# Row statistics of two layer norms in a Mamba block with FFN: from VectorE to ScalarE's accumulator output

## The chip, the cores and the metric

The kernel runs on one core of one Trainium2 chip. The time is device microseconds (us) of one execution on that core, given as the median of three runs; a profiled execution is a further run, with its own time. Five engines are in play, and the text uses the profile's names for them: PE (TensorE, matmuls), DVE (VectorE), ACT (ScalarE), POOL (GpSimd) and SP (SyncE, which issues the DMAs).

## The reference

The input x has shape (4, 2048, 256). The output is one pre-norm layer, a Mamba block and then a gated FFN, each in a residual connection. The change concerns only the two layer norms outside of the blocks; a third norm stands inside the Mamba block, and the kernel folds it into the first one.

```python
def _layernorm(x, axis=-1, eps=1e-05):
    m = jnp.mean(x, axis=axis, keepdims=True)
    v = jnp.var(x, axis=axis, keepdims=True)
    return (x - m) / jnp.sqrt(v + eps)
...
# _mamba_block(x, ...): D_INNER = 512, D_STATE = 64
mu = jnp.mean(x, axis=-1, keepdims=True)
var = jnp.mean(jnp.square(x - mu), axis=-1, keepdims=True)
xn = (x - mu) * jax.lax.rsqrt(var + 1e-05) * ln_w + ln_b
xz = xn @ W_in                       # xi, z; causal conv of width 4 on xi; u = silu(conv)
x_dbl = u @ W_xproj                  # dt_r, Bm, Cm;  delta = softplus(dt_r @ W_dt + b_dt)
def step(h, inputs):                 # one time step: h is (batch, 512, 64)
    d_t, B_t, C_t, u_t = inputs
    dA = jnp.exp(d_t[:, :, None] * A)
    h = h * dA + (d_t * u_t)[:, :, None] * B_t[:, None, :]
    y_t = jnp.einsum('bdn,bn->bd', h, C_t)
    return (h, y_t)
...                                  # y = (ys + u * D) * silu(z); return residual + y @ W_out
...
x = x + mamba(_layernorm(x))
x = x + ffn(_layernorm(x))           # ffn: (silu(x @ wg.T) * (x @ wu.T)) @ wd.T, weights from integers
```

## The kernel before

**Tiles and groups.** The 4 x 2048 tokens are cut into 16 tiles of 512 tokens, four to a sequence. The recurrence of a tile runs in 16 groups of 16 scans, so 256 scans a tile and 4096 in all. One scan is one DVE instruction over 512 time steps for 128 rows (two channels by 64 states). A group goes through this pipeline, all of it in `group`:

- SP loads `d*u` of 16 channel pairs, broadcast over the states, into a buffer of `ring` (three buffers of 128 x 16 x 512); four DMAs a group.
- POOL multiplies the ring by B in two instructions of eight rows each (`mul`, line 1578). Before that it puts the carried state into the first column (line 1451).
- For each pair, PE spreads delta over the rows by a matmul into one of four PSUM buffers `a` (line 1461), ACT takes the exponential in place (line 1467), and DVE runs the scan (line 1472), reading `a` and the ring's row and writing the ring's row.
- After the group, PE contracts the states with C in 64 "narrow" matmuls of 32 columns to a block of PSUM (line 1496), ACT evicts them (line 1517), PE permutes (line 1530). Only when the narrow matmuls have read the whole buffer can the ring's buffer be loaded for the group after the next two.

**Dense work.** What is not the recurrence is called dense: for tile n+1 `front` (loads x, both norms' statistics as one, normalises, transposes), `front_a` (projection, convolution), `front_b` (projection of z, a block of three SiLU activations between two table loads at lines 947 to 950, softplus, stores of what the recurrence loads); for tile n-1 `back` (gate, output projection, residual, store of the sum x1 to DRAM, `rsum`) and `back_b` (loads x1 again, norm of the FFN, FFN with a SiLU block at lines 1198 to 1200, residual, store). All of it runs beside the scans of tile n. The first tile's front and the last tile's end (`back_early`, `back_last`) stand outside.

**The norm.** `layer_norm` takes for each of four blocks of 128 tokens a `bn_stats` over 256 values and a `bn_aggr` (lines 469 and 470, both DVE), which give mean and variance in a PSUM buffer `lp`. ACT adds eps (line 479), takes Ln and Exp (489, 490) and a square (491); three small DVE instructions (494, 499, 504) finish the reciprocal root by a Newton step and make the bias -mean times that. `normalise` (line 520) is one ACT instruction a block, with a scale and a bias from SBUF. The norm is called 16 times in `front` (with `twice=True`), 15 times in `back_b`, and twice for half a tile in `back_last`.

**The order.** No engine reorders its instructions. `Planner.run` writes the order of every queue when the kernel is built: it steps through the operations with a cost that the kernel states for each, places on each engine what can start first, and biases dense work by a due step. A changed cost or operation thus moves other operations too. PSUM has four buffers `ps` for everything but `a`; SBUF has four of `w4` and eight small ones `s4`. Where it judges that PE has had little work lately, the planner issues a matmul of line 1461 twice.

Of the kernel before, what the change touches and what calls it, by code (L numbers as in the profile page):

```python
# [15 lines left out]
AF = mybir.ActivationFunctionType  # L16
# [4 lines left out]
P = 128  # L21
# [35 lines left out]
TINY = 60  # L57
SWITCH = 90
PAD = 0.0
SLACK = {"DVE": 300.0, "POOL": 300.0}  # L60


# [29 lines left out]
class Planner:  # L92
# [13 lines left out]
    def buf(self, tag):  # L106
        tag, view = self.alias.get(tag, (tag, None))
        t = tag if tag in self.ordered else tag + self.kind
        b = Buf(tag, self.turns.get(t, 0), view)
        self.turns[t] = b.turn + 1  # L110
        return b
# [225 lines left out]
def mamba_ffn_kernel(  # L337
# [81 lines left out]
    def act(n=T, psum=False, ptr=0):  # L419
        return n * 0.834 + (70 if psum else 110) + 93 * ptr  # L420
# [23 lines left out]

        return t[:, b // 2, b % 2 : b % 2 + 2, :].rearrange("p a c -> p (a c)")

    def layer_norm(src, blocks=range(4), twice=False):

        nb = len(blocks)
        m = 2 if twice else 1
        lp, ve, rs, nm = buf("ps"), buf("s4"), buf("s4"), buf("s4")

        def sq():
            return lp.t[:, 16 : 16 + m * nb]

        def col(b):
            return b.t[:, 0 : m * nb]

        def mv():
            return lp.t[:, 0 : 2 * nb].rearrange("p (s c) -> p s c", c=2)

        def two(v):
            return v.rearrange("p (m s) -> p m s", m=m)

        def stats(j, s):
            st = buf("bst")
            op("DVE", 326, lambda: nc.vector.bn_stats(st.t, tok(src)[:, s, :]), [(src, s // 2)], [st])
            op("DVE", 205, lambda: nc.vector.bn_aggr(mv()[:, j, :], st.t), [st], [(lp, 0, j)])  # L470

        for j, s in enumerate(blocks):
            stats(j, s)
        mk = [(lp, 0, j) for j in range(nb)]

        def var(i):
            op(
                "ACT", 180,
                lambda: nc.scalar.activation(
                    ve.t[:, i * nb : (i + 1) * nb], mv()[:, :, 1], AF.Copy,  # L480
                    bias=EPS * EPS if i else EPS, scale=1.0 + EPS if i else 1.0,
                ),
                mk, [(ve, i)],
            )

        for i in range(m):
            var(i)
        vk = [(ve, i) for i in range(m)]
        op("ACT", 180, lambda: nc.scalar.activation(col(rs), col(ve), AF.Ln), vk, [rs])
        op("ACT", 180, lambda: nc.scalar.activation(col(rs), col(rs), AF.Exp, scale=-0.5), [rs], [rs])  # L490
        op("ACT", 180, lambda: nc.scalar.activation(sq(), col(rs), AF.Square), [rs], [(lp, 1)])
        op(
            "DVE", TINY,
            lambda: nc.vector.scalar_tensor_tensor(sq(), sq(), -0.5, col(ve), ALU.mult, ALU.mult),
            [(lp, 1)] + vk, [(lp, 1)],
        )
        op(
            "DVE", TINY,
            lambda: nc.vector.scalar_tensor_tensor(col(rs), sq(), 1.5, col(rs), ALU.add, ALU.mult),
            [(lp, 1), rs], [rs],  # L500
        )
        op(
            "DVE", TINY,
            lambda: nc.vector.scalar_tensor_tensor(  # L504
                two(nm.t[:, 0 : m * nb]), mv()[:, None, :, 0].to_broadcast([P, m, nb]), -1.0,
                two(rs.t[:, 0 : m * nb]), ALU.mult, ALU.mult,
            ),
            mk + [rs], [nm],
        )
        return rs, nm  # L510

# [193 lines left out]

    B2, yts, heads_in = {}, {}, {}

    rest, gates, last = {}, {}, {}

    def load_x(n):  # L710
        b, q = n // NQ, n % NQ
# [9 lines left out]
    def front(n):  # L721
        r = n % R
        xt = load_x(n) if n else x0
        rs, nm = layer_norm(xt, twice=True)
        rp = buf("s4")
        op("ACT", 180, lambda: nc.scalar.activation(rp.t[:, 0:4], rs.t[:, 0:4], AF.Copy, bias=1.0), [rs], [rp])
        xn = buf("w4")
        normalise(xn, xt, (rs, nm), o=4)

        def keep():  # L730
            normalise(xt, xt, (rp, nm))
            store(rsum[r], lambda: tok(xt), 524288, halves(xt), [("rsum", r)])

        if n:
            keep()
        else:
            last["keep"] = keep
        xnT = buf("w4")

        def ev_t(c):  # L740
            def ev(ps):
                op(
                    "ACT", act(T, True, 2),
                    lambda: nc.scalar.activation(  # L744
                        xnT.t[:, c, :], ps.t, AF.Identity, bias=lnb[:, c : c + 1], scale=lnw[:, c : c + 1]
                    ),
                    [ps, "lnw", "lnb"], [(xnT, c)],
                )

            return ev  # L750

        for c in range(2):
            transposes(xn, c, ev_t(c))
        rest[n] = xnT
# [349 lines left out]
            ),  # L1104
        )

    def residual(pieces, reads, x1, h):

        ps = buf("ps")
        v = lambda: tok(x1)[:, h * 2 : h * 2 + 2, :].rearrange("p s c -> p (s c)")  # L1110
        open_bank(ps)
        op("ACT", act(), lambda: nc.scalar.copy(ps.t, v()), [(x1, h), ps], [ps])
        for cost, f in pieces:
            op("PE", cost, lambda f=f: f(ps.t), reads, [ps])
        op("ACT", act(T, True), lambda: nc.scalar.copy(v(), ps.t), [ps], [(x1, h)])

    def ev_add(x1, h):
        def ev(ps):
# [13 lines left out]
    def back(n):  # L1132
        r = n % R
        b, q = n // NQ, n % NQ
        y2 = buf("w8")
        for hf in range(2):
            for rh in range(2):
                ld = [buf(("yl", "w2")[rh]) for _ in range(2)]
                for _ in gate_y(n, y2, hf, rh, ld):
                    pass  # L1140
        x1 = buf("w4")
        load(lambda: tok(x1), rsum[r], 524288, r=[("rsum", r)], w=[(x1, 0), (x1, 1)])

        for h in range(2):
            yk = [(y2, hf, h) for hf in range(2)]
            residual(
                [mm_tok_add(wout, lambda k: y2.t[:, k, :], s, k, range(4)) for s in (2 * h, 2 * h + 1) for k in range(4)],
                yk + ["wout"], x1, h,
            )
        store(rsum[r], lambda: tok(x1), 524288, halves(x1), [("rsum", r)])  # L1150

    def back_b(n):
        r = n % R
        b, q = n // NQ, n % NQ
        x1 = buf("w4")
        load(lambda: tok(x1), rsum[r], 524288, r=[("rsum", r)], w=halves(x1))
        sc = layer_norm(x1)
        xn = buf("w4")
        normalise(xn, x1, sc)
        xT = buf("w4")  # L1160

        def ev_t(c):
            def ev(ps):
                op("ACT", act(T, True), lambda: nc.scalar.copy(xT.t[:, c, :], ps.t), [ps], [(xT, c)])

            return ev

        for c in range(2):
            transposes(xn, c, ev_t(c))
        hma, hmb = buf("w8"), buf("w4")  # L1170

        def hm(k):
            return hma.t[:, k, :] if k < 4 else hmb.t[:, k - 4, :]

        hk = [(hma, k) for k in range(4)] + [(hmb, k) for k in range(2)]

        def ev_g(k):
            def ev(ps):
                op("ACT", act(T, True), lambda: nc.scalar.copy(hm(k), ps.t), [ps], [hk[k]])

            return ev

        def ev_u(k):
            def ev(ps):
                up = buf("w2")
                op("ACT", act(T, True), lambda: nc.scalar.copy(up.t, ps.t), [ps], [up])  # L1186
                op(
                    "POOL", 1230, lambda: nc.gpsimd.tensor_tensor(hm(k), hm(k), up.t, ALU.mult),  # L1188
                    [up, hk[k]], [hk[k]],
                )  # L1190

            return ev

        for k in range(6):
            project(wgu, k * P, xT, ev_g(k), [("wgu", 0, k)])

        def silu():
            nc.scalar.activation(hma.t, hma.t, AF.Silu)
            nc.scalar.activation(hmb.t, hmb.t, AF.Silu)
            nc.scalar.preload_act_table_set(EXP_LN)  # L1200

        op("ACT", 5450, silu, hk, hk).tail = -1283.0
        for k in range(6):
            project(wgu, HID + k * P, xT, ev_u(k), [("wgu", 1, k)])
        wdk = [("wd", c, k) for c in range(2) for k in range(3)]
        for h in range(2):
            residual(
                [mm_tok_add(wd, hm, s, k, range(6)) for s in (2 * h, 2 * h + 1) for k in range(6)],
                hk + wdk, x1, h,
            )  # L1210
        store(
            out[b, q * T : (q + 1) * T, :].rearrange("(s p) c -> p s c", p=P), lambda: tok(x1), 524288,
            [(x1, 0), (x1, 1)], [],
        )
# [436 lines left out]
```

## Time and profile before

| | |
|---|---|
| median of three runs | 5000.17 us (4996.33 to 5005.06) |
| the profiled execution, its own time | 4990.98 us |
| its span in the profile | 4989.2 us |
| granted TensorE clock | 0.98 |
| DVE busy | 4758.8 us (95%) |
| POOL busy | 4697.7 us (94%) |
| PE busy | 4475.7 us (90%) |
| ACT busy | 3973.4 us (80%) |
| DVE scans, line 1472 | 4595.0 us, 4096 instructions |
| POOL multiplications, line 1578 | 4545.0 us, 512 instructions |
| DVE `bn_stats`, line 469 | 45.1 us, 128 instructions |
| DVE `bn_aggr`, line 470 | 21.8 us, 128 instructions |

Busy time is the time in which an engine runs at least one instruction; neighbours on one engine overlap a little, so an instruction's own duration (1195 ns for a scan) is longer than the distance to the next one. In the groups' lines, the columns are the line, engine, operation, output and inputs with shapes, the count, the busy time and mean duration, and the idle time of the engine just before, with what ended it. In the timeline each line has a start, a duration, the engine, line, operation and count of a run of equal instructions, and in brackets the idle time before it.

### The profile page before, as it was taken

What the parts mean: (1) busy time and instruction counts of PE and PEld (TensorE: products, weight loads), DVE (VectorE), ACT (ScalarE), POOL (GpSimd) and SP (SyncE); (2) the same over time, 40 slices, a digit from 0 to 9 for tenths busy, and PEclk for the clock granted to TensorE, in tenths of its full rate; (3) what the DMA queues carried; (4) which work ended last, traced back from release to release, by engine and by line L of the source; (5) the groups of instructions that cost most, each with busy time, mean ns of one, the idle gap of its engine ahead of it and who ended that gap; (6) DMA issues with size and microseconds to landing.
All of it is one profiled execution on the core that took longest, in us unless ns stands there. A gap on an engine that the chain in (4) does not pass through costs nothing.

```text
span 4989.2 us, 115894 instructions
## 1 busy us (share of the span) xinstructions
PE 4475.7 (90%) x46955; PEld 2171.1 (44%) x46955; DVE 4758.8 (95%) x4696; ACT 3973.4 (80%) x7138; POOL 4697.7 (94%) x862
## 2 busy tenths in 40 slices
PE   7889899899988989989998989989999898899888
PEld 2434344444444444444443434434444343444435
DVE  7999999999999999999999999999999999999996
ACT  6778878788787887878878787887878878788674
POOL 6999999999999999999999999999999999999994
PEclk9999999999999999999999999999999999999999
DMA  8676676666676767767667666667767677676762
GB/s 291 236 280 269 262 281 262 259 271 254 263 289 255 273 235 271 296 260 272 250 267 278 259 253 251 271 270 273 268 261 276 234 271 290 243 277 246 266 252 85
DMA packets 306346, 1299.86 MB, mean 261 GB/s; under 512 B 33617, under 2 KB 134737, under 8 KB 174866
## 3 DMA queue, kind: packets, MB, share of 16 engines
q1 hardware_dynamic: 305810, 1292.44, 67.3%
q8 instruction: 369, 6.05, 0.5%
q14 instruction: 167, 1.37, 0.1%
HBM read 1186.94 MB, written 105.38 MB: 259 GB/s over the span
## 4 chain that ended last, share of the span: by engine, by line
PE 41%; DVE 20%; ACT 15%; issue 10%; DMA 8%; POOL 5%; DVEq 0%; SPq 0%; POOLq 0%; ACTq 0%
DVE ring L1472 19%; PE a L1461 11%; PE ps L1496 9%; ACT a L1467 7%; PE ps L545 7%; DMA ring<-dusc 4%; PE ps L1097 4%; POOL ring L1578 4%; PE ps L779 3%; DMA yl<-qd 2%; PE ps L1530 2%; PE ps L898 2%; ACT mm L1517 1%; DMA dusc<-w 1%; PE ps L846 1%
## 5 line engine op out<-in xcount | busy, mean ns | idle before, releaser
L1578 POOL TENSOR_TENSOR ring<-ring,b 128x4088 f32<-128x4088 f32 (+2 forms) x512 | 4545.0, 8920 | 177.0 <-DMA ring<-dusc 110.3
L1472 DVE TENSOR_TENSOR_SCAN ring<-a,ring 128x512 f32<-128x512 f32 x4096 | 4595.0, 1195 | 104.9 <-ACT a L1467 62.5
L1467 ACT ACTIVATE a<-a,a 128x512 f32<-128x512 f32 x4096 | 2697.0, 665 | 707.3 <-PE a L1461 678.0
L1461 PE MATMUL a<-stk,selb 128*128 128x512 bf16 x5119 | 1806.7, 388 | 417.0 <-DVE ring L1472 376.5
L1496 PE MATMUL ps<-ring,cz 128*32 128x128 f32 x32768 | 1288.6, 279 | 11.1 <-issue 6.6
L1496 PEld LDWEIGHTS ps<-ring,cz 128*32 128x32 f32 x32768 | 786.3, 109 | 756.1 <-issue 699.2
L1461 PEld LDWEIGHTS <-selb 128*128 128x128 bf16 x5119 | 474.5, 98 | 1302.5 <-issue 1223.8
L545 PE MATMUL ps<-w,wgu 128*128 128x512 f32 x720 | 378.1, 608 | 0.0
L1517 ACT COPY mm<-ps 128x512 f32<-128x512 f32 x512 | 303.7, 593 | 53.0 <-PE ps L1496 52.0
L1530 PE MATMUL ps<-mm,exs 128*32 128x128 f32 (+1 forms) x4112 | 285.5, 407 | 5.8 <-ACT mm L1517 5.7
L545 PE MATMUL ps<-w,win 128*128 128x512 f32 x512 | 264.4, 601 | 0.3 <-ACT w L744 0.3
L779 PE MATMUL ps<-xi,w 128*128 128x512 f32 x480 | 248.6, 599 | 0.0
L1530 PEld LDWEIGHTS ps<-mm,exs 128*32 128x32 f32 x4112 | 117.3, 119 | 185.6 <-ACT a L1467 82.8
L1097 PE MATMUL ps<-wd,w 128*128 128x256 f32 x720 | 195.2, 387 | 0.0
L545 PEld LDWEIGHTS ps<-w,wgu 128*128 128x128 f32 x720 | 138.5, 194 | 103.9 <-issue 50.3
L1097 PEld LDWEIGHTS ps<-wd,w 128*128 128x128 f32 x720 | 132.5, 190 | 39.1 <-issue 12.7
L898 PE MATMUL ps<-w,ident 128*128 128x512 f32 x248 | 132.7, 618 | 2.8 <-ACT w L878 1.2
L1188 POOL TENSOR_TENSOR w<-w,w 128x512 f32<-128x512 f32 x90 | 114.6, 1301 | 16.0 <-ACT w L1186 15.8
L1097 PE MATMUL ps<-wout,w 128*128 128x256 f32 x480 | 128.8, 383 | 0.0
L545 PEld LDWEIGHTS ps<-w,win 128*128 128x128 f32 x512 | 96.6, 192 | 71.9 <-issue 48.8
L1041 PE MATMUL ps<-prm,yt 128*128 128x128 f32 x512 | 83.7, 294 | 34.6 <-ACT ps L1054 34.0
L520 ACT ACTIVATE w<-w,s,s 128x256 f32<-128x256 f32 x192 | 112.2, 592 | 1.9 <-DVE s L504 0.9
(147 smaller groups left out, 2381.9 us busy)
## 6 DMA issues: line engine op xcount, KB each, us to landing
ring<-dusc SPq DMA_DIRECT2D x1023, 1024.0 KB, 8.3
stk<-dsc SPq DMA_DIRECT2D x256, 96.0 KB, 5.5
qd<-w SPq DMA_DIRECT2D x32, 512.0 KB, 5.6
szd<-w SPq DMA_DIRECT2D x32, 512.0 KB, 8.3
dusc<-w SPq DMA_DIRECT2D x63, 256.0 KB, 3.6
dsc<-pk SPq DMA_DIRECT2D x63, 256.0 KB, 3.0
rsum<-w SPq DMA_DIRECT2D x31, 512.0 KB, 3.4
w<-rsum SPq DMA_DIRECT2D x31, 512.0 KB, 7.9
```

What stands on the lines that cost most here:

```text
L545: lambda ps: nc.tensor.matmul(ps, w[:, c, o : o + P], xT.t[:, c, :], start=(c == 0), stop=(c == 1)),
L779: lambda: nc.tensor.matmul(ps.t, dg.t[:, j * P : (j + 1) * P], xi.t[:, j : j + T], start=(j == 0), stop=(j == 3)),
L898: lambda: nc.tensor.matmul(ps.t, m, t.t, start=False, stop=True, skip_group_check=True),
L1097: lambda ps: nc.tensor.matmul(ps[:, (s % 2) * DM : (s % 2 + 1) * DM], src(k)[:, s * P : (s + 1) * P], w[:, k, :], start=False, stop=(k == ...
L1188: "POOL", 1230, lambda: nc.gpsimd.tensor_tensor(hm(k), hm(k), up.t, ALU.mult),
L1461: "PE", 216, lambda: nc.tensor.matmul(a.t, selb[:, p, :], stk.t, start=True, stop=True),
L1467: lambda: nc.scalar.activation(a.t, a.t, AF.Exp, scale=a2f[:, idx : idx + 1]), [a, "a2"], [a],
L1472: nc.vector.tensor_tensor_scan(v, a.t, v, 0.0, ALU.mult, ALU.add)
L1496: nc.tensor.matmul(pm.t[cg * 32 : cg * 32 + 32, (r8 % 4) * P : (r8 % 4 + 1) * P], framed(cz, blk), ring.t[:, :, blk * 8 : blk * 8 + 8], st ...
L1517: nc.scalar.copy(mm.t[:, hb * 4 : hb * 4 + 4].rearrange("p r a t -> p (r a t)"), pm.t)
L1530: nc.tensor.matmul(ex.t[jh * 32 : jh * 32 + 32, a * 16 : b * 16], framed(exs, jh * 2 + jl), mm.t[:, a:b, :, jh * 2 + jl], start=(jl == 0), ...
L1578: e.tensor_tensor(v, v, b2.t[:, None, t0:].to_broadcast([P, m, T - t0]), ALU.mult)
```

## The change

The fifteen inner tiles' norms of both kinds no longer use `bn_stats` and `bn_aggr`. ACT sums instead, by the output `accum_out` of an activation.

- In `front` of tiles 1 to 15, a new function `sums_of` runs four copies of a 128 x 256 block into a PSUM buffer that nobody reads, each with its row sums as a second output. `layer_norm` then scales the sums to -mean (one small ACT instruction) and runs four `Square` activations with -mean as a bias from SBUF, whose row sums are 256 times the variance.
- In `back` the eviction of the residual (two copies of 128 x 512) becomes four of 128 x 256 with row sums. The rest of the norm's scalars is worked out there, from x1 while it lies in SBUF; `back_b` only loads x1 and normalises.
- The first tile's front and the two half norms at the end stay as they are.
- The planner is told 60 ns more for an instruction with an accumulator output (`ACC`).

```diff
+ACC = 60.0
...
+    def sums_of(src):
+        sums = buf("s4")
+        sink = buf("ps")
+        def one(s):
+            op("ACT", act(DM) + ACC,
+                lambda: nc.scalar.activation(
+                    sink.t[:, 0:DM], tok(src)[:, s, :], AF.Copy, accum_out=sums.t[:, s : s + 1]),
+                [(src, s // 2)], [sink, (sums, s)])
...
-    def layer_norm(src, blocks=range(4), twice=False):
+    def layer_norm(src, blocks=range(4), twice=False, sums=None):
...
+        def spread(s):
+            op("ACT", act(DM, ptr=1) + ACC,
+                lambda: nc.scalar.activation(
+                    lp.t[:, DM : 2 * DM], tok(src)[:, s, :], AF.Square,
+                    bias=sums.t[:, 4 + s : 5 + s], accum_out=sq4.t[:, s : s + 1]),
+                [(src, s // 2), (sums, 4)], [(lp, 2), (sq4, s)])
...
+        if sums is None:
+            for j, s in enumerate(blocks):
+                stats(j, s)
+        else:
+            op("ACT", 180,
+                lambda: nc.scalar.activation(sums.t[:, 4:8], sums.t[:, 0:4], AF.Copy, scale=-1.0 / DM),
+                [(sums, s) for s in range(4)], [(sums, 4)])
+            for s in range(4):
+                spread(s)
...
     def front(n):
-        rs, nm = layer_norm(xt, twice=True)
+        rs, nm = layer_norm(xt, twice=True, sums=sums_of(xt) if n else None)
...
-    def residual(pieces, reads, x1, h):
+    def residual(pieces, reads, x1, h, sums=None):
-        op("ACT", act(T, True), lambda: nc.scalar.copy(v(), ps.t), [ps], [(x1, h)])
+        if sums is None:
+            op("ACT", act(T, True), lambda: nc.scalar.copy(v(), ps.t), [ps], [(x1, h)])
+            return
+        def one(i):
+            s = h * 2 + i
+            op("ACT", act(DM, True) + ACC,
+                lambda: nc.scalar.activation(
+                    tok(x1)[:, s, :], ps.t[:, i * DM : (i + 1) * DM], AF.Copy, accum_out=sums.t[:, s : s + 1]),
+                [ps], [(x1, h), (sums, s)])
...
     def back(n):
+        sums = buf("s4")
...
         store(rsum[r], lambda: tok(x1), 524288, halves(x1), [("rsum", r)])
+        norms[n] = layer_norm(x1, sums=sums)
     def back_b(n):
         load(lambda: tok(x1), rsum[r], 524288, r=[("rsum", r)], w=halves(x1))
-        sc = layer_norm(x1)
-        normalise(xn, x1, sc)
+        normalise(xn, x1, norms[n])
```

More of the change, by code (lines that the diff above doesn't have):

```diff
@@ L445, in framed @@
         return t[:, b // 2, b % 2 : b % 2 + 2, :].rearrange("p a c -> p (a c)")
-    def layer_norm(src, blocks=range(4), twice=False):
+    def sums_of(src):
+        sums = buf("s4")
+        sink = buf("ps")
+        def one(s):
+            op(
+                "ACT", act(DM) + ACC,
+                lambda: nc.scalar.activation(
+                    sink.t[:, 0:DM], tok(src)[:, s, :], AF.Copy, accum_out=sums.t[:, s : s + 1]
+                ),
+                [(src, s // 2)], [sink, (sums, s)],
+            )
+        for s in range(4):
+            one(s)
+        return sums
+    def layer_norm(src, blocks=range(4), twice=False, sums=None):
         nb = len(blocks)
         m = 2 if twice else 1
-        lp, ve, rs, nm = buf("ps"), buf("s4"), buf("s4"), buf("s4")
+        lp = buf("ps")
+        sq4 = buf("s4") if sums else None
+        ve, rs, nm = buf("s4"), buf("s4"), buf("s4")
         def sq():
@@ L470, in stats, with var_in, minus_mean @@
             op("DVE", 205, lambda: nc.vector.bn_aggr(mv()[:, j, :], st.t), [st], [(lp, 0, j)])
-        for j, s in enumerate(blocks):
-            stats(j, s)
-        mk = [(lp, 0, j) for j in range(nb)]
+        def spread(s):
+            op(
+                "ACT", act(DM, ptr=1) + ACC,
+                lambda: nc.scalar.activation(
+                    lp.t[:, DM : 2 * DM], tok(src)[:, s, :], AF.Square,
+                    bias=sums.t[:, 4 + s : 5 + s], accum_out=sq4.t[:, s : s + 1],
+                ),
+                [(src, s // 2), (sums, 4)], [(lp, 2), (sq4, s)],
+            )
+        if sums is None:
+            for j, s in enumerate(blocks):
+                stats(j, s)
+            mk = [(lp, 0, j) for j in range(nb)]
+        else:
+            op(
+                "ACT", 180,
+                lambda: nc.scalar.activation(sums.t[:, 4:8], sums.t[:, 0:4], AF.Copy, scale=-1.0 / DM),
+                [(sums, s) for s in range(4)], [(sums, 4)],
+            )
+            for s in range(4):
+                spread(s)
+            mk = [(sq4, s) for s in range(4)]
+        def var_in():
+            return mv()[:, :, 1] if sums is None else sq4.t[:, 0:4]
+        def minus_mean():
+            return mv()[:, None, :, 0] if sums is None else sums.t[:, None, 4:8]
         def var(i):
@@ L479, in var @@
                 lambda: nc.scalar.activation(
-                    ve.t[:, i * nb : (i + 1) * nb], mv()[:, :, 1], AF.Copy,
-                    bias=EPS * EPS if i else EPS, scale=1.0 + EPS if i else 1.0,
+                    ve.t[:, i * nb : (i + 1) * nb], var_in(), AF.Copy,
+                    bias=EPS * EPS if i else EPS, scale=(1.0 + EPS if i else 1.0) / (1 if sums is None else DM),
                 ),
@@ L504, in layer_norm @@
             lambda: nc.vector.scalar_tensor_tensor(
-                two(nm.t[:, 0 : m * nb]), mv()[:, None, :, 0].to_broadcast([P, m, nb]), -1.0,
+                two(nm.t[:, 0 : m * nb]), minus_mean().to_broadcast([P, m, nb]), 1.0 if sums else -1.0,
                 two(rs.t[:, 0 : m * nb]), ALU.mult, ALU.mult,
             ),
-            mk + [rs], [nm],
+            (mk if sums is None else [(sums, 4)]) + [rs], [nm],
         )
@@ L706, in mamba_ffn_kernel @@
     B2, yts, heads_in = {}, {}, {}
-    rest, gates, last = {}, {}, {}
+    rest, gates, norms, last = {}, {}, {}, {}
     def load_x(n):
@@ L1114, in residual @@
             op("PE", cost, lambda f=f: f(ps.t), reads, [ps])
-        op("ACT", act(T, True), lambda: nc.scalar.copy(v(), ps.t), [ps], [(x1, h)])
+        if sums is None:
[3 more added lines that the diff above has]
+            s = h * 2 + i
+            op(
+                "ACT", act(DM, True) + ACC,
+                lambda: nc.scalar.activation(
+                    tok(x1)[:, s, :], ps.t[:, i * DM : (i + 1) * DM], AF.Copy, accum_out=sums.t[:, s : s + 1]
+                ),
+                [ps], [(x1, h), (sums, s)],
+            )
+        for i in range(2):
+            one(i)
     def ev_add(x1, h):
@@ L1147, in back @@
                 [mm_tok_add(wout, lambda k: y2.t[:, k, :], s, k, range(4)) for s in (2 * h, 2 * h + 1) for k in range(4)],
-                yk + ["wout"], x1, h,
+                yk + ["wout"], x1, h, sums,
             )
         store(rsum[r], lambda: tok(x1), 524288, halves(x1), [("rsum", r)])
+        norms[n] = layer_norm(x1, sums=sums)
     def back_b(n):
```

## The prediction

> **What bounds the kernel now.** I read the page's busy shares first, then the groups by line, then the timelines of DVE and ACT over one inner tile, then who waited for whom.
>
> ```profile
> PE 4475.7 (90%) x46955; PEld 2171.1 (44%) x46955; DVE 4758.8 (95%) x4696; ACT 3973.4 (80%) x7138; POOL 4697.7 (94%) x862
> ```
>
> DVE is the fullest engine, POOL is almost as full. The groups say what fills DVE and what the change takes away:
>
> ```profile
> L1472 DVE TENSOR_TENSOR_SCAN ring<-a,ring 128x512 f32<-128x512 f32 x4096 | 4595.0, 1195 | 104.9 <-ACT a L1467 62.5 <-POOL ring L1451 34.5 <-POOL ring L1578 7.7
> L469 DVE BATCH_NORM_STATS2 bst<-w 128x6 f32<-128x256 f32 x128 | 45.1, 410 | 26.6 <-DMA w<-rsum 24.8 <-DMA w<-in 1.7
> L470 DVE BATCH_NORM_AGGREGATE ps<-bst 128x2 f32<-128x6 f32 x128 | 21.8, 170 | 1.3
> ```
>
> Read alone, this looks like 67 us of DVE work and 25 us of waiting for a reload to be had. The timeline shows where that work stands. First DVE, in two stretches of one tile, then ACT beside the first:
>
> ```profile
> 1324.40 74.77 DVE L1472 TENSOR_TENSOR_SCAN ring<-a,ring 128x512 f32<-128x512 f32 x67
> 1400.27 1.41 DVE L469 BATCH_NORM_STATS2 bst<-w 128x6 f32<-128x256 f32 x4 [1.09 <-DMA w<-rsum]
> 1403.69 22.39 DVE L1472 TENSOR_TENSOR_SCAN ring<-a,ring 128x512 f32<-128x512 f32 x20 [2.02 <-ACT a L1467]
> ...
> 1482.66 0.39 DVE L470 BATCH_NORM_AGGREGATE ps<-bst 128x2 f32<-128x6 f32 x2
> ...
> 1489.95 29.07 DVE L1472 TENSOR_TENSOR_SCAN ring<-a,ring 128x512 f32<-128x512 f32 x26
> 1518.95 0.47 DVE L1391 TENSOR_TENSOR ps<-ps,a 128x128 f32<-128x128 f32 x2
> 1519.33 1.39 DVE L469 BATCH_NORM_STATS2 bst<-w 128x6 f32<-128x256 f32 x4
> 1522.11 36.89 DVE L1472 TENSOR_TENSOR_SCAN ring<-a,ring 128x512 f32<-128x512 f32 x33 [1.39 <-ACT a L1467]
> 1560.54 17.94 DVE L1472 TENSOR_TENSOR_SCAN ring<-a,ring 128x512 f32<-128x512 f32 x16 [1.54 <-POOL ring L1578]
> ```
>
> ```profile
> 1395.72 0.67 ACT L1467 ACTIVATE a<-a,a 128x512 f32<-128x512 f32 x1
> 1396.41 1.28 ACT L947 ACT_TABLE_LOAD   x1
> 1397.71 1.91 ACT L947 ACTIVATE w<-w 128x2048 f32<-128x2048 f32 x1
> 1399.53 1.99 ACT L949 ACTIVATE w<-w 128x1024 f32<-128x1024 f32 x2
> 1401.53 1.28 ACT L950 ACT_TABLE_LOAD   x1
> 1402.83 0.27 ACT L1539 COPY yt<-ps 128x128 f32<-128x128 f32 x1
> ```
>
> Sixty-seven scans take 74.77 us, so one follows the other every (74.77 - 1.19) / 66 = 1.115 us. The scans are the spine: the first starts at 54.7 us, 4096 x 1.115 = 4567 us, the last ends at 4933.1 us, and 56 us of tail follow. That leaves 4989.2 - 54.7 - 4567 - 56 = 311 us in which DVE does something else between scans or waits. Only that can move.
>
> The SiLU block keeps ACT from exponentials from 1396.4 to 1402.8 us. DVE uses up the (at most four) finished `a` buffers, runs dry at 1399.2 and resumes at 1403.7: a hole of 4.5 us. All four `bn_stats` stand in it, the wait for the reload too, and DVE still waits 2.02 us for ACT after them. The second block (line 1198) makes a hole of about 3 us, and the front's four `bn_stats` stand there, again with ACT coming last. In the order of the instructions 29 of the 30 inner norms lie like this: their `bn_stats` follow the last scan whose exponential precedes a SiLU's table load.
>
> **The change part by part.** All terms stand against the profiled execution (4990.98 us); the median of the runs is 9.2 us above it, and I carry the difference over to the median.
>
> *The 120 `bn_stats` and the waits for the reload.* 42.3 us busy (45.1 x 120/128) and 24.8 us of waits, of which I count nothing as gain: the SiLU block covers them, and what comes next in the hole is ACT's exponential at the same moment as now. Without that cover they would be worth 67 us.
>
> *The 120 `bn_aggr`.* From 1482.66 to 1489.95 us, 7.29 us hold six scans (6.69 us), four `bn_aggr` and three small operations that stay; a scan with one of the latter takes 1.19 us instead of 1.115. So four `bn_aggr` cost 7.29 - 6.69 - 3 x 0.07 = 0.4 us, 30 norms 12 us. The front's stand between 1578 and 1593 us, where the rows around them wait 0.84 and 0.22 us for POOL; a faster DVE would wait longer there. Between 6 and 12 us, I take -9.
>
> *New work on ACT.* The trace has no accumulating activation. Nearest rows for the instruction itself: 0.37 us for a 128x256 copy (lines 1262 and 1277), 0.49 us for a 128x256 activation with one operand from SBUF (1054), 0.20 us for a tiny one. A front gets 4 x 0.37 + 4 x 0.49 + 0.20 = 3.6 us, a back 4 x 0.37 - 2 x 0.59 + 4 x 0.49 + 0.20 = 2.5 us; fifteen of each 92 us. The second output costs between nothing (the same pass over the data; it can't be less) and a small instruction of its own (0.19 us for 128x3, line 771): 240 times, 0 to 46 us. I take 20 us, nearer to the first, as nothing moves but one value a row. ACT goes from 3973 to some 4085 us, 82%. Is it on the path? In the new order the squares stand one behind each exponential: 0.60 + 0.49 + 0.02 to 0.19 us against a scan's 1.115 us, so at worst ACT falls back 0.2 us a block, 1.6 us a norm, against a lead of up to three scans (3.3 us). The norms stand 50 and more exponentials ahead of the SiLU blocks, and just ahead of those the new order has less dense work on ACT than the old. So 0; if the lead were gone, the 1.6 us of 30 norms would cost 48 us. The copies and squares use functions that lines 491 and 726 already run between the same table loads; no load is added.
>
> The Trainium skill speaks against this move: its page "ScalarE: Activation LUTs", section "Rules for kernel authors", says to put additions and multiplications on VectorE, which is the quicker engine for them. Rows agree on the engine time (1.41 + 0.4 us on DVE against 2.5 to 3.6 us on ACT), and if engine time were what counts, the sum would be 92 - 54 = 38 us slower, about 5038. But the rule weighs the engines as if both were on the path.
>
> *Waits that move.* The reload of x1 is now waited for by ACT's normalise, with the exponentials queued behind it; DVE waited up to 3.1 us for it. SP issues it at the same place of its queue, and on ACT the first normalise stands eight exponentials behind the SiLU block, over 8 us later than `bn_stats` stood. 0. `sums_of` holds one of four `ps` buffers for four copies, and `lp` is held through the squares; on SP no DMA is added or removed.
>
> *The moved order.* The planner's costs changed, so everything dense shifts: the order has 104 doubled matmuls of line 1461 fewer (104 x 0.39 = 40 us of PE, none on the path). What matters is when a group's narrow matmuls are through, since the reload of its ring buffer waits for the last. In the tile shown, the group whose scans end at 1540.9 had them through only at 1562.5, with FFN matmuls in between; POOL waited 4.2 us, and DVE then 1.54 us at 1560.54. DVE's waits for POOL are 34.5 + 7.7 = 42 us in all. Counted in matmuls of line 1461 between a group's end and its last narrow matmul, groups 12 and 13 of a tile go from 20.2 and 19.4 to 16.9 and 18.4, but groups 5 to 8 from 14.6, 13.5, 12.6, 14.6 to 19.0, 15.3, 13.5, 13.9; the mean goes from 14.4 to 14.0. Bounds: -42 us (all such waits gone) to +42 us (a second such place); I take -9, a fifth of the waits, as the worst place gets better and another nearly as bad appears.
>
> Sum: 0 - 9 + 0 - 9 = -18 us, so 4973 us for the profiled execution and 5000.2 - 18 = 4982 us for the median.
>
> **The rivals.**
>
> *Full relief.* DVE gets all of it: 42.3 + 12 + 24.8 = 79 us less, 4921 us. For it speaks the 95%; against it that the row after the stats waits for ACT, not the other way.
>
> *Nothing to measure.* The back's aggregates come (-6), the front's are lost to POOL, and the moved order takes a few us: 4990 to 5010 us.
>
> *Slower: PE late at a second place.* Groups 5 to 8 now have their narrow matmuls late. A buffer that is free d us after its group's scans end is loaded and landed 5 us later, POOL starts about 3 us after that and needs 8.9 us for the first half; two groups of scans give 2 x 17.9 = 35.7 us. So DVE waits once d exceeds some 19 us, counted here as about 19 matmuls, just where group 5 now stands. POOL is in order and has no reserve (94%), so a loss stays. Price: as at the present place, up to 42 us, with the gain from the aggregates 33 us net: 5010 to 5035 us.
>
> **How the numbers follow.** The likeliest case (4965 to 4990 us) gets 0.47, full relief 0.08, nothing 0.20, slower 0.25. A run of this kernel can be told from no change at about 0.2%, 10 us. Faster by more: 0.47 + 0.08, less 0.01 for the edge, 0.54; same 0.20; slower 0.26. Below 4960 us lies full relief and a corner of the likeliest (0.10), above 5028 us the upper part of the slower case (0.10); between them 0.8.
>
> **What would show it.** Right: the holes at the SiLU blocks keep their 4.5 and 3 us; DVE's wait for `a` from ACT rises from 62.5 us by about the removed 42 and 25 us, to some 125 us, while DVE busy falls to about 4700 us; ACT busy is 4065 to 4110 us; DVE's waits for POOL are some 33 us. Wrong: the holes shrink (full relief), the waits of line 1472 for POOL rise over 50 us (the slower rival), or waits for `a` appear away from the SiLU blocks, which would mean that accumulating costs ACT far more than 0.19 us.

## The result, and the profile after

The changed kernel takes 5204.61 us (median of four runs, 5182.04 to 5245.78) against 4999.86 us before (four runs): 1.0421 times as long, with a 95% interval of 1.0388 to 1.0453. That is 205 us slower, where 18 us faster was forecast and 5028 us was the upper end of the range. The profiled execution was the fastest of the four, 5182.04 us; its span is 5180.3 us.

First the busy shares on the page of the changed kernel:

```profile
PE 4464.3 (86%) x46549; PEld 2178.5 (42%) x46851; DVE 4883.3 (94%) x4456; ACT 4051.3 (78%) x7618; POOL 4695.3 (91%) x862
```

DVE has 240 instructions fewer (4456 against 4696) and is busy 124.5 us longer. So an instruction that stayed has become dearer. The groups by line, with different shapes kept apart, name it. The first two lines are of the kernel before, the last of the norm's three small operations (the 16 of the front include the first tile); the others are of the changed kernel, where the same operation stands in line 551:

```profile
L504 DVE SCALAR_TENSOR_TENSOR s<-ps,s 128x8 f32<-128x8 f32 x16 | 2.2, 139 | 0.0
...
L504 DVE SCALAR_TENSOR_TENSOR s<-ps,s 128x4 f32<-128x4 f32 x15 | 2.0, 133 | 0.0
```

```profile
L1535 DVE TENSOR_TENSOR_SCAN ring<-a,ring 128x512 f32<-128x512 f32 x4096 | 4593.8, 1197 | 170.3 <-ACT a L1530 135.9 <-issue 19.6 <-POOL ring L1514 10.9
...
L551 DVE SCALAR_TENSOR_TENSOR s<-s,s 128x8 f32<-128x8 f32 x15 | 104.0, 6934 | 0.2
...
L551 DVE SCALAR_TENSOR_TENSOR s<-s,s 128x4 f32<-128x4 f32 x15 | 72.3, 4822 | 0.0
```

An operation on four or eight values a row went from 0.14 us to 6.9 and 4.8 us: 176.3 us in 30 instructions. Its idle time before is nil, so by the column on the right it waits for nothing; the time lies inside of the instruction. The operands differ: `s<-ps,s` before (one input in PSUM), `s<-s,s` now (both in SBUF). The timeline shows what ends it. First DVE, then POOL in the same microseconds:

```profile
1071.53 1.21 DVE L1535 TENSOR_TENSOR_SCAN ring<-a,ring 128x512 f32<-128x512 f32 x1
1072.66 8.33 DVE L551 SCALAR_TENSOR_TENSOR s<-s,s 128x4 f32<-128x4 f32 x1
1080.92 2.33 DVE L1535 TENSOR_TENSOR_SCAN ring<-a,ring 128x512 f32<-128x512 f32 x2
```

```profile
1063.31 17.66 POOL L1641 TENSOR_TENSOR ring<-ring,b 128x4088 f32<-128x4088 f32 x2
1080.87 0.26 POOL L1514 COPY ring<-carry 128x16 f32<-128x16 f32 x1
```

The small operation begins at 1072.66 and ends at 1080.99 us; POOL's second multiplication ends at 1080.97. All 30 inner instances end like this, within 0.1 us behind the end of a POOL instruction. In the first tile, where POOL is idle and the operand still in PSUM, the operation took 0.17 us. Four of the 30 do not get through at the end of the POOL instruction that was running. One of these, 2.77 us long, got through 0.4 us behind it, at the end of a small POOL operation; the other three last through the ends of two or three multiplications: 16.8, 24.7 and 24.7 us. One of these, DVE and then POOL:

```profile
2594.28 24.70 DVE L551 SCALAR_TENSOR_TENSOR s<-s,s 128x8 f32<-128x8 f32 x1
```

```profile
2574.91 44.03 POOL L1641 TENSOR_TENSOR ring<-ring,b 128x4096 f32<-128x4096 f32 x5
```

The chain of waits then leads on: ACT's normalise needs the operation's result, and the exponentials are queued behind it. The waits of the changed kernel (total, times, longest):

```profile
DVE ring L1535 <- ACT a L1530: 135.9, 55, 5.3
ACT w L567 <- DVE s L551: 100.1, 12, 24.4
```

### The profile page after: what moved, and what is told of

The parts are those of the page before. It is cut to its first block, busy times and chain, and to the rows that moved or that the text cites. A ratio compares the mean times of both kernels' runs of the same rounds, so it can differ in the third digit from the quotient of the medians.

```text
span 5180.3 us, 115594 instructions
## 1 busy us (share of the span) xinstructions
PE 4464.3 (86%) x46549; PEld 2178.5 (42%) x46851; DVE 4883.3 (94%) x4456; ACT 4051.3 (78%) x7618; POOL 4695.3 (91%) x862
## 5 line engine op out<-in xcount | busy, mean ns | idle before, releaser
L1641 POOL TENSOR_TENSOR ring<-ring,b 128x4088 f32<-128x4088 f32 (+2 forms) x512 | 4537.2, 8885 | 325.8 <-DMA ring<-dusc 172.2
L1535 DVE TENSOR_TENSOR_SCAN ring<-a,ring 128x512 f32<-128x512 f32 x4096 | 4593.8, 1197 | 170.3 <-ACT a L1530 135.9
L1524 PE MATMUL a<-stk,selb 128*128 128x512 bf16 x4738 | 1725.7, 389 | 546.5 <-DVE ring L1535 522.3
L1559 PE MATMUL ps<-ring,cz 128*32 128x128 f32 x32768 | 1311.7, 281 | 26.7 <-issue 3.7
L551 DVE SCALAR_TENSOR_TENSOR s<-s,s 128x8 f32<-128x8 f32 (+1 forms) x30 | 176.3, 5878 | 0.2
L826 PEld LDWEIGHTS ps<-xi,w 128*128 128x128 f32 x480 | 89.1, 193 | 80.5 <-issue 70.4
```

The costliest lines, as they stand in the source:

```text
L551: lambda: nc.vector.scalar_tensor_tensor(two(nm.t[:, 0 : m * nb]), minus_mean().to_broadcast([P, m, nb]), 1.0 if sums else -1.0, two(rs.t[ ...
L826: lambda: nc.tensor.matmul(ps.t, dg.t[:, j * P : (j + 1) * P], xi.t[:, j : j + T], start=(j == 0), stop=(j == 3)),
L1524: "PE", 216, lambda: nc.tensor.matmul(a.t, selb[:, p, :], stk.t, start=True, stop=True),
L1535: nc.vector.tensor_tensor_scan(v, a.t, v, 0.0, ALU.mult, ALU.add)
L1559: nc.tensor.matmul(pm.t[cg * 32 : cg * 32 + 32, (r8 % 4) * P : (r8 % 4 + 1) * P], framed(cz, blk), ring.t[:, :, blk * 8 : blk * 8 + 8], st ...
L1641: e.tensor_tensor(v, v, b2.t[:, None, t0:].to_broadcast([P, m, T - t0]), ALU.mult)
```

## The experiments

The theory after the first look at the traces (A in the expectations): the operand's place is the cause, not the sums on ACT and not the new order. Its rivals (B and C) were that the moved order makes somebody late, or that ACT with its accumulators does. Times in the comparisons stand against the kernel before on the same chip: 4998.12 us for the first four kernels, 4995.01 for the next four, 4998.0 for the last. Behind each time stand the ratio to the kernel before and its 95% interval in brackets.

### The changed kernel in the same order, the operand in PSUM

ACT writes -mean to `lp` too, in the same planned step as the first square, so that the order stays the changed kernel's; only the small operation's input moves.

```diff
 def spread(s):
+    if s == 0: nc.scalar.activation(lp.t[:, 32:36], sums.t[:, 4:8], AF.Copy)
     nc.scalar.activation(lp.t[:, DM : 2 * DM], ..., AF.Square, ...)
 def minus_mean():
-    return mv()[:, None, :, 0] if sums is None else sums.t[:, None, 4:8]
+    return mv()[:, None, :, 0] if sums is None else lp.t[:, None, 32:36]
```

> The changed kernel, in which -mean is also copied into PSUM (one more ScalarE instruction of 0.2 us a norm, 30 in all), so that the last small VectorE operation (line 551 of the changed kernel) reads -mean from PSUM instead of SBUF; every queue keeps its order. Theory A (an operation with both inputs in SBUF waits until GpSimd's running multiplication has ended): the 30 operations take 0.14 us each again instead of 5.9 us, their 176 us and the waits behind them go, and the time is 4970 to 5010 us. Theory B (the accumulating activations and their reads make ScalarE late): no change, 5190 to 5210 us. Theory C (the moved order of the dense work): no change either, over 5150 us.

Measured: 5000.95 us, 1.0008 [0.9998, 1.0019]. Busy shares and the operation's groups (line 552 here):

```profile
PE 4474.1 (89%) x46851; PEld 2163.0 (43%) x46851; DVE 4709.8 (94%) x4456; ACT 4050.6 (81%) x7648; POOL 4695.2 (94%) x862
```

```profile
L552 DVE SCALAR_TENSOR_TENSOR s<-ps,s 128x8 f32<-128x8 f32 x16 | 2.4, 150 | 0.2
...
L552 DVE SCALAR_TENSOR_TENSOR s<-ps,s 128x4 f32<-128x4 f32 x15 | 2.0, 133 | 0.0
```

The spans differ by 5180.3 - 4999.3 = 181.0 us, the operation's busy time by 172 us (176.3 against the 4.4 here, which include the first tile's); by the medians the two kernels differ by 204 us. The order, the sums on ACT and the accumulators are all still there. So both rivals fall, and the operand is the cause.

### The kernel before, with the operand in SBUF

The other direction: nothing of the change, its order untouched, but ACT copies the means to SBUF, and the small operation reads them there.

```diff
+    if i == 0: nc.scalar.activation(mc[:, 0:nb], mv()[:, :, 0], AF.Copy)
...
-    two(nm.t[:, 0 : m * nb]), mv()[:, None, :, 0].to_broadcast([P, m, nb]), -1.0,
+    two(nm.t[:, 0 : m * nb]), mc[:, None, 0:nb].to_broadcast([P, m, nb]), -1.0,
```

> The kernel before, statistics on VectorE as they were and every queue in its order; ScalarE copies the four means from PSUM to SBUF (0.2 us a norm) and the last small VectorE operation (line 504 of the kernel before) reads them there, so that both its inputs lie in SBUF. Theory A: 30 such operations meet a multiplication of 8.9 us at any point of it and wait 3 to 6 us each: 5090 to 5180 us. Theories B and C: 4995 to 5010 us, no change, since no sum is made on ScalarE and nothing is moved.

Measured: 5149.86 us, 1.0309 [1.0287, 1.0331], 152 us more by the medians. The groups of this kernel (`dm` is the SBUF tile that holds the means):

```profile
L506 DVE SCALAR_TENSOR_TENSOR s<-dm,s 128x4 f32<-128x4 f32 x15 | 105.3, 7017 | 0.0
...
L506 DVE SCALAR_TENSOR_TENSOR s<-dm,s 128x8 f32<-128x8 f32 x16 | 63.9, 3995 | 0.0
...
L506 DVE SCALAR_TENSOR_TENSOR s<-dm,s 128x2 f32<-128x2 f32 x2 | 0.3, 160 | 0.1
```

Together 169.2 us where it was 4.2. The two instances at the very end, where POOL has nothing left to do, take 0.16 us with the same operands. In the middle of the run three instances fall into moments in which POOL was idle, and take 0.13 to 0.14 us. One of them on DVE, and POOL around it, whose first multiplication here ends at 2155.13:

```profile
2155.30 0.13 DVE L506 SCALAR_TENSOR_TENSOR s<-dm,s 128x4 f32<-128x4 f32 x1
```

```profile
2146.20 8.93 POOL L1580 TENSOR_TENSOR ring<-ring,b 128x4088 f32<-128x4088 f32 x1
2156.49 8.88 POOL L1580 TENSOR_TENSOR ring<-ring,b 128x4088 f32<-128x4088 f32 x1 [1.36 <-DMA ring<-dusc]
```

So both inputs in SBUF alone cost nothing, only beside POOL.

### The repair as a step of its own

As in the first experiment, but planned as its own ACT operation of 180 ns, which gives a new order.

```diff
+    op("ACT", 180, lambda: nc.scalar.activation(lp.t[:, 32:36], sums.t[:, 0:4], AF.Copy, scale=-1.0 / DM),
+        [(sums, s) for s in range(4)], [(lp, 4)])
...
-    return mv()[:, None, :, 0] if sums is None else sums.t[:, None, 4:8]
+    return mv()[:, None, :, 0] if sums is None else lp.t[:, None, 32:36]
```

> The same repair, but the copy into PSUM is an operation of its own that the planner knows of (180 ns), so the whole order of the queues is planned anew. Theory A: 4970 to 5010 us, as with the old order. Theory C: it differs from the repair with the old order by more than 20 us, one way or the other, since a new order is drawn.

Measured: 4975.86 us, 0.9964 [0.9952, 0.9975]. This beats both kernels. It differs from the first experiment by little but the order, and that is worth 25 us; below this is looked at again.

### The kernel before, each `bn_stats` twice

```diff
-    op("DVE", 326, lambda: nc.vector.bn_stats(st.t, tok(src)[:, s, :]), ...)
+    op("DVE", 326, twice_over, ...)   # the same bn_stats two times
```

> The kernel before with each bn_stats made twice, in place, every queue in its order: 128 more VectorE instructions, 45 us more busy time. Of the prediction's step that the SiLU holes cover the statistics: the time rises by no more than 0 to 10 us (the two ends have no cover, 8 x 0.35 us), and VectorE's wait for the exponentials falls from 62.5 us to about 25 us. Of its rival that VectorE's busy time counts: 5040 to 5050 us.

Measured: 5012.84 us, 1.0030 [1.0018, 1.0042]. DVE's busy time rose by 54.1 us, the kernel by 15, more than the 10 expected at most. DVE's waits for `a` fell from 62.5 to 32.9 us. So most of the added work went into the holes at the SiLU blocks. The hole that the prediction shows is just filled: behind the eighth `bn_stats` the next scan waits 0.26 us for ACT, where it was 2.02. Part of the rest is what no longer fits. In eight other holes, where the reload comes late, the `bn_stats` now end last, and these holes last 5.48 us on average, where they lasted 4.74; in ten holes of the front's norms they end last too, 3.67 us against 3.24, some 10 us in all. The 13 holes that ACT still ends kept their length.

### The kernel before, `bn_stats` over 8 of 256 values

The statistics are taken over the first 8 values of a row only; the other 248 are left out. The order is that of the kernel before.

```diff
-    op("DVE", 326, lambda: nc.vector.bn_stats(st.t, tok(src)[:, s, :]), ...)
+    op("DVE", 326, lambda: nc.vector.bn_stats(st.t, tok(src)[:, s, 0:8]), ...)
```

> The kernel before with every queue in its order, where bn_stats reads 8 of the 256 values of a row (the statistics are left out in the main): some 0.25 us less for each of 128 instructions, 32 us less VectorE work. If the SiLU holes cover the statistics: 0 to 4 us less, 4994 to 5000 us, and VectorE's wait for the exponentials rises by about 30 us. If VectorE's busy time counts: 4965 to 4970 us.

Measured: 4998.18 us, 1.0003 [0.9993, 1.0012]. DVE's busy time fell by 31.9 us, and one row of its waits took the time:

```profile
DVE ring L1472 <- ACT a L1467: 102.9, 43, 3.8
```

That is 40.4 us more than the 62.5 of before. The work of `bn_stats` on DVE costs nothing, as forecast.

### One half of the repaired change alone

The repaired kernel, with the sums on ACT in the front alone (the back as before), and in the back alone.

```diff
 # front only, in back and back_b:
-        norms[n] = layer_norm(x1, sums=sums)
...
+        sc = layer_norm(x1)
...
 # back only, in front:
-        rs, nm = layer_norm(xt, twice=True, sums=sums_of(xt) if n else None)
+        rs, nm = layer_norm(xt, twice=True)
```

> The repaired kernel (-mean copied to PSUM by an operation that the planner knows of), with the sums on ScalarE in front alone; the FFN's norm is as in the kernel before. If the gain of 22 us comes from the bn_aggr that go (0.4 us a norm), half of the norms bring about half of it: 4985 to 4990 us. If it comes from the newly planned order, it can be anything between 4965 and 5010 us.

Measured: 5041.45 us, 1.0090 [1.0075, 1.0105], above both ranges that were expected. DVE waited 35.2 + 10.5 us for POOL, and its product in line 958 waited 48 us for ACT; in the whole repaired kernel these are 15.1 + 4.5 and 32.7 us.

> The same with the sums on ScalarE in back alone; front's statistics stay on VectorE. By the bn_aggr that go: 4985 to 4990 us. By the newly planned order: anything between 4965 and 5010 us.

Measured: 5014.95 us, 1.0034 [1.0020, 1.0048], above both ranges too.

Both halves are slower than before, the whole is faster (0.9964). Parts of a sum cannot behave so: each of the three has an order of its own, so these runs do not price either half.

### The same instructions, other orders

To see what an order is worth, kernels whose instructions differ only in sequence: the planner is told another price. Twice in the repaired kernel (`ACC` 200 and 100 instead of 60) and twice in the kernel before.

```diff
-ACC = 60.0
+ACC = 200.0     # and 100.0
...
-    op("DVE", 326, lambda: nc.vector.bn_stats(...
+    op("DVE", 350, lambda: nc.vector.bn_stats(...
...
-    op("DVE", 205, lambda: nc.vector.bn_aggr(...
+    op("DVE", 190, lambda: nc.vector.bn_aggr(...
```

> The repaired kernel with ACC = 200, about what the read of the accumulator took in the profile (0.20 us), instead of 60. If the planner's wrong price costs anything, VectorE's waits for ScalarE (lines of the scan and of delta times u) fall and the time is 4950 to 4970 us; if not, it is another order of the same quality, 4965 to 4990 us.

Measured: 5035.64 us, 1.0076 [1.0061, 1.0091], above both ranges that were expected. DVE waited 46.1 + 20.4 us for POOL and 146.7 us for `a`.

> The repaired kernel (-mean copied to PSUM by an operation of its own) with ACC = 100, between the 60 (4976 us) and the 200 (5036 us) that were run. If the planner's price for the accumulating instruction is what costs, the time lies between the two; if the order is a draw, anywhere from 4970 to 5040 us.

Measured: 4983.32 us, 0.9966 [0.9953, 0.9979].

> The kernel before, every instruction as it was, but the planner is told 350 ns instead of 326 for bn_stats, so that it draws another order (some 1100 rows of the queues differ). If an order is worth about as much as the next: within 10 us of before. If a new order alone moves the time as the five repaired variants differed: up to 40 us, either way, and more likely up, since the order of before is the one that was kept.

Measured (350 for `bn_stats`): 5011.46 us, 1.0027 [1.0018, 1.0036].

> The same with 190 instead of 205 ns for bn_aggr (some 800 rows differ): as above, 4990 to 5035 us, and not the same time as the other redrawn order.

Measured (190 for `bn_aggr`): 4994.11 us, 0.9994 [0.9984, 1.0004].

So an order alone is worth up to some tens of us. In the kernel before, a price 24 ns higher cost 13 us, and another one 15 ns lower moved the time by 4 us, not clear of noise. In the repaired kernel, prices of 60, 100 and 200 gave 4976, 4983 and 5036 us. These three rise with the price, so they do not tell chance from an effect of the price; but the price nearest to what the chip takes (0.20 us for an accumulator read, see below) gave the slowest. Why one order is better was not taken apart further than the rows above.

### The changed kernel, POOL's multiplications in halves

If the small operation only waits for the running POOL instruction, instructions of half the length should halve the wait. The operand stays in SBUF.

```diff
-        e.tensor_tensor(v, v, b2.t[:, None, t0:].to_broadcast([P, m, T - t0]), ALU.mult)
+        for i in range(0, m, 4):
+            ...   # the same on four of the rows: v[:, i : i + k]
```

> The changed kernel as given (-mean in SBUF), every queue in its order, but GpSimd multiplies four rows at a time instead of eight, so that one multiplication takes some 4.5 us instead of 8.9. If line 551 waits until the running multiplication has ended, its mean falls from 5.9 us to about 3 us or less, and no instance ends inside of a multiplication that ran when it began. If it waits for a fixed time, or until GpSimd has a pause, it stays at 5 to 6 us. The whole time: 5204 us less up to 90 us, plus some 45 us for the added instructions of GpSimd if they count.

Measured, in one run: 5233.15 us. The groups of the operation, then one instance on DVE and POOL beside it:

```profile
L551 DVE SCALAR_TENSOR_TENSOR s<-s,s 128x8 f32<-128x8 f32 x15 | 136.8, 9121 | 0.2
...
L551 DVE SCALAR_TENSOR_TENSOR s<-s,s 128x4 f32<-128x4 f32 x15 | 103.5, 6897 | 0.0
```

```profile
1071.78 10.51 DVE L551 SCALAR_TENSOR_TENSOR s<-s,s 128x4 f32<-128x4 f32 x1
```

```profile
1068.85 13.43 POOL L1644 TENSOR_TENSOR ring<-ring,b 128x2044 f32<-128x2044 f32 x3
```

The wait did not halve: it rose from 5.9 to (136.8 + 103.5) / 30 = 8.0 us. The operation shown sat past the ends of two halves and got through at the third, and the three longest lasted 25 to 27 us, past five or six ends. So it waits not simply for the running instruction. It always gets through at the end of one, and five of the six longest waits here, like the three longest in the changed kernel, ended ahead of a stretch of 9 us and more in which POOL had nothing to do. What decides at which end it gets through stays open.

## Why the prediction was wrong, by its own steps

**The step that failed** is a half sentence in the part on the aggregates: "three small operations that stay", at 0.07 us each beside a scan. Two of them stayed. The third, the bias, kept its place and its shape, but the change gives it -mean from `sums` (SBUF) in place of the mean from `lp` (PSUM). I priced an operation by its name and size and did not compare its operands. Ahead of the time that it then takes stands no wait that the view of waits could name, so of the signs that I listed only DVE's busy time shows it, 4883 instead of about 4700 us; the holes, the waits for POOL and ACT's busy time do not. (The waits for `a` away from the SiLU blocks came as well, but they stand in the run with the operand put back too; see below.) The forecast of that step was 30 x 0.07 = 2 us, the runs show 176 us, and 181 us by the spans when only the operand is put back.

The rows say: two SBUF inputs beside a POOL multiplication 5.9 us, one PSUM input beside it 0.13 to 0.15 us, two SBUF inputs without POOL 0.13 to 0.16 us. The Trainium skill has the rule behind it: its page "SBUF — State Buffer", section "Who interferes with whom", says that a VectorE instruction with two SBUF inputs contends with a GpSimd instruction that reads SBUF, and that one with at most one SBUF input, outside of VectorE's two-port modes, does not. The rows agree, the scan with `a` in PSUM among them: in the kernel before it took 1.195 us beside POOL and 1.195 us in the 71 scans that met no POOL instruction. The page's summary has the later one blocked until the first finishes; the halves of the last experiment show waits past the ends of up to six POOL instructions, and there the measurement decides.

**The statistics and the holes: right.** `bn_stats` was to be worth nothing. Leaving nearly all of it out gave 1.0003, and doubling it cost 15 us of 54. The hole of 4.5 us stands in the changed kernel too, now empty:

```profile
1455.50 19.06 DVE L1535 TENSOR_TENSOR_SCAN ring<-a,ring 128x512 f32<-128x512 f32 x17 [4.64 <-ACT a L1530]
```

DVE's waits for `a` were to rise from 62.5 to some 125 us (by my own terms, 62.5 + 42 + 25, to 130); the row shows 135.9 us, and 136.8 in the run with the operand put back. In that run a second row belongs to them, as four of its five waits stand at SiLU blocks, of 4.3 to 4.5 us like the others there:

```profile
DVE ring L1536 <- ACT a L1531: 136.8, 55, 4.6
...
DVE ring L1536 <- issue: 18.1, 5, 4.5
```

Both rows sorted by place: at the SiLU blocks (from the first table load to 5 us behind the second) the waits rose from 51.4 to 115.4 us, by 64 us where 67 were forecast. Away from them they rose from 11.1 to 39.6 us, which was not. In that run DVE is busy 4709.8 us, about the 4700 forecast. Full relief (4921 us) is refuted.

**The new work on ACT: a term off in size, and waits that were put at nothing.** I took 20 us for 240 accumulator outputs, between 0 and 46. It is a separate instruction each time. From the groups of the changed kernel:

```profile
L496 ACT ACTIVATION_READ_ACCUMULATOR ps<-w,s 128x1 f32 x120 | 23.8, 198 | 0.0
...
L1170 ACT ACTIVATION_READ_ACCUMULATOR w<-ps 128x1 f32 x60 | 12.6, 210 | 0.0
...
L456 ACT ACTIVATION_READ_ACCUMULATOR ps<-w 128x1 f32 x60 | 11.8, 197 | 0.0
```

Together 48.2 us, the upper bound and a little more. Still ACT's busy time is 4051 us, below the 4065 to 4110 forecast: I had added up durations, and neighbours on ACT overlap (all ACT durations together rose by 145 us, the busy time by 78). The work did not decide: with all of it in place, the operand put back makes 1.0008. But "So 0" for its place on the path was not what the trace shows. Of the signs of being wrong one came, waits for `a` away from the SiLU blocks, 28.5 us more of them, and with them 25.3 us more of waits for two ACT evictions (next paragraph). I had read that sign as accumulating at far more than 0.19 us, which it is not, at 0.20 us. Whether the added work or the new order makes these waits stays open: kernels without the sums have 11 to 24 us of waits away from the blocks, three that keep the order of before 17 to 23 us; kernels with the sums in both norms have 22 to 40 us, those with the sums in one norm 33 and 58 us. The rule of the page "ScalarE: Activation LUTs", section "Rules for kernel authors", on keeping additions and multiplications on VectorE, priced by the rows' engine time, would have made it about 5038 us; 5001 and 4976 us with the repair speak against weighing it so here.

**The aggregates and the order: open by what an order is worth.** With the operand put back, the sum was to be -18 us; it is +3 us (5000.95 against 4998.12) in the changed kernel's order, and +10 us between the two spans (4989.2 and 4999.3), of which the parts can be read. DVE's busy time falls by 49.0 us (4758.8 to 4709.8) and the reload's 24.8 us are gone, while the waits at the SiLU blocks rise by 64.0 us: together -9.8 us, as the first two terms of my sum had it (0 - 9). DVE's waits for POOL fall by 24.0 us (42.2 to 18.2), more than the 9 us that I counted. Against these stand the 28.5 us away from the blocks and 25.3 us of waits of the product in line 954 (line 906 before) for two ACT evictions; the rest fell by 10.5 us.

```profile
DVE w L954 <- ACT x L958: 26.5, 14, 4.2
DVE w L954 <- ACT pk L953: 18.3, 7, 5.9
```

It was 14.2 + 5.3 us before. I had followed the exponentials on ACT and not these evictions.

I had put the moved order at -9 within ±42 us, and by a place that I misread. The narrow matmuls that were through only at 1562.5 us cannot have made POOL's wait of 4.2 us nor DVE's of 1.54 us, which had ended by then (at 1525.64 and 1560.54). What stands behind 1562.5 is a wait of 0.94 us:

```profile
1525.64 8.88 POOL L1578 TENSOR_TENSOR ring<-ring,b 128x4096 f32<-128x4096 f32 x1 [4.22 <-ACT x L1400]
...
1570.28 8.92 POOL L1578 TENSOR_TENSOR ring<-ring,b 128x4088 f32<-128x4088 f32 x1 [0.94 <-DMA ring<-dusc]
```

Kernels with the same instructions lay 22 us below (`ACC` 60) to 41 us above (`ACC` 200) the kernel before, so the bounds were fair and the middle means little. The slower rival (POOL late at a second place) is not what happened: DVE waited 10.9 + 3.6 us for POOL in the changed kernel.

That the repaired kernel at 4976 us comes near the forecast of 4982 is therefore in part luck of the order, and no proof of its terms.

## What to carry to other kernels

When a change moves an operand from PSUM to SBUF, price the instructions that read it anew, however small: beside a POOL that is 94% busy with SBUF data, an operation of 0.14 us with both inputs in SBUF took 5.9 us and held the fullest engine. Look in the diff for every operand whose memory changes, not only for instructions added and removed, and keep one input of such an operation in PSUM. Where a planner writes the order, measure a few orders with the same instructions before giving a per cent to the edit.

## What the runs showed of the hardware that was not expected

- A DVE instruction with two SBUF inputs beside back-to-back POOL multiplications of 8.9 us: 27 of 30 took 4.1 us on average ((176.3 - 66.2) / 27), close to half a multiplication, and three took 16.8 to 24.7 us. With POOL's instructions cut to 4.5 us the mean rose to 8.0 us and the longest to 27.0 us. Idle time before such an instruction is nil; the wait is inside of its duration. POOL loses nothing (its multiplications took 4537.2 us, before 4545.0).
- An activation with an accumulator output is two instructions on ACT; the read of the accumulator takes 0.20 to 0.21 us for one value a row, about half as long as the 128x256 copy (0.39 us) that it belongs to.
